# An LSTM over 512 steps: 18 instead of 19 plain steps in the head, U sums ahead of cells, raw V blocks stored later

## The chip, the cores and the metric

The kernel runs on one core of a Trainium2 chip. The metric is the device time of one execution in microseconds, the median of the runs. In names of engines, PE is TensorE, DVE is VectorE, ACT is ScalarE, POOL is GpSimd and SP is SyncE, whose queue issues all DMAs here.

## The reference

An LSTM layer with residual, batch 32, 512 steps, input and hidden size 512, float32:

```python
xW = jnp.einsum('ntd,dg->ntg', x, Wx) + b          # 32 x 512 x 2048
def step(carry, xw_t):
    prev_h, prev_c = carry
    a = xw_t + prev_h @ Wh
    i = jax.nn.sigmoid(a[:, :Hd])
    f = jax.nn.sigmoid(a[:, Hd:2 * Hd])
    o = jax.nn.sigmoid(a[:, 2 * Hd:3 * Hd])
    g = jnp.tanh(a[:, 3 * Hd:])
    next_c = f * prev_c + i * g
    next_h = o * jnp.tanh(next_c)
    return ((next_h, next_c), next_h)
return x + lstm_forward(x, cond_1024, Wx, Wh, b)   # cond_1024 is h0; c0 = 0
```

## The kernel before, in words

**Two kinds of work share PE.** The serial one: in each step t, `h_part(t)` multiplies h by Wh (32 matmuls into one PSUM bank, L272), and `cell(t)` does the gates: ACT L285 to L290 and DVE L288 to L292 in the head, ACT L298 to L305 and DVE L302 to L309 later; the transposed h (`ht`, L292 or L309) releases h_part(t + 1). POOL adds the residual (L317), and SP stores two steps' output (L321). While a cell runs, PE is filled with the other work, x times Wx.

**x times Wx in two ways.** 32 of the 512 steps are *plain*: 32 matmuls of 128x256 each (`plain_block`, L200). `HEAD` of them come first (steps 0 to 18 before), `TAIL` of them are the last steps of the sequence (13 before). The other 480 steps go in 15 *groups* of 32 by a bilinear scheme: 26 products ("slots") per group instead of 32, and each of these again by a 7-item scheme. An item is 8 matmuls (L593) and is counted as 4 *quarters*, so that a group has 26 x 7 x 4 = 728 quarters. The variable `pos` is the place in the list of items; `emit_matmuls(n)` writes n quarters.

**What the bilinear products need.** Left factors are sums of x blocks: pair sums (`pair_sum`, DVE L538 to L544) over rows of x that SP loads (`load_row`, L528), and above them *U sums* (`make_sum`, DVE L507, into one of a few `ubuf` buffers, list `free_u`). `u_ahead(n)` makes all U sums for products up to n quarters ahead. Right factors are *V sums* of Wx blocks (`v_sum`, DVE L784 and L787), made once in the head, stored to DRAM (L791) and loaded row by row into a ring of three (`load_v`, L706 for blocks taken raw from Wx, L711 for stored ones). Blocks that are raw (`V_DIRECT`) are taken from Wx at first, and copied once into the DRAM table by `store_raw` (L688), three copies per block, one per step from a given step on. For eight blocks these are 24 steps.

**What comes behind the products.** `evacuate()` takes finished items out of PSUM: copies by ACT (L659, L668, L675) and adds by DVE (L665, L669, L672). *Weight sums* (`w_op`, DVE L451, 128x1024) combine slots into output blocks in the buffers `cbuf`, `r` and one spare (buffer 9) that lies in `xnat`. `store_blocks` stores a finished block (SP L469), and `load_xw` (SP L735, four DMAs a step) brings back the x times Wx of a step two or three steps later, which ACT copies into the step's PSUM bank (L746). Biases are seeded into banks by ACT (L636).

**The order of work is written out by hand.** Each engine runs its instructions in the order of the code. In the head, `HEAD_PLAINS[t]` names the plain steps computed in step t ahead of need, `HEAD_STREAM[t]` the quarters of the first group in step t, and `jobs[t]` the DVE work of the first steps. In a step with 48 quarters or more from step 10 on (`late_cell`), two chunks of 12 and 24 quarters are written ahead of the cell, and the rest behind it; the last branch before `emit_matmuls` in the loop decides which U sums and weight sums are written in each chunk. A budget `room["dve"]` in estimated ns steers the weight sums. From step `HEAD_STEPS` = `HEAD` on a fixed rule spreads 22 to 24 quarters over each step. At the end, from step `END`, the plain steps of the tail are computed in pieces (`plain_part`, L209), 16 pieces a plain step, five pieces per step from `SPLIT` on, as long as there are any; from `SPLIT` on gates are split in halves.

Of the kernel before, what the change touches and what calls it, by code (L numbers as in the profile page):

```python
# [20 lines left out]
W = G * P  # L21
HW = G * H

HEAD = 19
GS = 32
NG = 15
TAIL = T - HEAD - NG * GS
# [10 lines left out]
STREAM0 = HEAD + GS - AHEAD  # L38
END = HEAD + GS * NG - AHEAD
SPLIT = END + 2  # L40
LATE = (452, 454, 456, 462, 464, 466, 467)

FIRST = 13
HEAD_PLAINS = ((14, 15), (16, 17), (18, 5), (6, 11), (12,), (), (7,), (8,), (9,), (10,))
HEAD_STREAM = (0, 0, 0, 0, 0, 24, 52, 52, 56, 56, 60, 60, 60, 60, 60, 56, 52, 44, 36)
HELD = 4
V_DIRECT = (2, 3, 7, 8, 15, 17, 21, 24)

# [57 lines left out]
def kernel(  # L106
# [228 lines left out]
    free_u = [2, 3, 0, 1, 4, 5]  # L335
# [197 lines left out]
    def pair_sum(g, qs):  # L533
        z = pairs_at(min(PLACES[g % 2][q] for q in qs), len(qs))
        a21, a11, a12, a22, s1, s2, s3, s4 = (z[:, :, n] for n in range(8))
        i = group(g).summed[qs[0]]
        if i == 0:
            add(s1, a21, a22)  # L538
        elif i == 1:
            sub(s2, s1, a11)  # L540
        elif i == 2:
            sub(s3, a11, a21)
        else:
            sub(s4, a12, s2)  # L544
        for q in qs:
            group(g).summed[q] += 1
        room["dve"] -= cost_dve(256 * len(qs))
# [329 lines left out]
    with tc.manual_schedule():  # L877
# [56 lines left out]
        jobs = {}  # L934
        sums = lambda *ids: [lambda i=i: v_sum(i) for i in ids]
        jobs[0] = sums(13, 14, 15, 16)
        jobs[1] = sums(17, 18, 19) + [make_seeds] + sums(20)
        jobs[2] = sums(21, 22, 23)
        jobs[3] = [lambda: pair_sum(0, (0, 1))] * 4 + sums(24)
        jobs[4] = [lambda: u_ahead(8)] + sums(25) + [lambda: u_ahead(24)]  # L940
        raws = lambda *ids: [lambda s=s: v_raw(s) for s in ids]
        jobs[5] = [lambda: u_ahead(40)] + raws(0, 7, 17, 24)
# [21 lines left out]
        for t in range(T):  # L964
# [12 lines left out]
            if last_x and t == last_x[0] + 3:  # L977
                load_x(NCHUNK - 1)
            assert last_x or t < SPLIT - 4
            if HEAD - 2 <= t < HEAD - 2 + 3 * len(V_DIRECT):  # L980
                s, d = divmod(t - HEAD + 2, 3)
                store_raw(V_DIRECT[s], d)
            if t == 2:
                load_row(0, 0)
# [12 lines left out]
            if t < HEAD_STEPS:  # L997
# [22 lines left out]
                for i, (kind, m, cs) in enumerate(chunks):  # L1020
                    if kind == "plain":
                        room["dve"] = max(room["dve"], 0.0) + PLAIN * len(cs) / 4
                        for cc in cs:
                            plain_block(m, cc, plain_bank(m), True)
                        if i == 0:
                            cell(t)
                        evacuate()
                        if cs[-1] == 3:
                            keep(m, True)
                        plains -= 1  # L1030
                        for _ in range(-(-len(todo) // (plains + 1))):
                            todo.pop(0)()
                            flush_v()
                        if not plains:
                            for f in ends.get(t, ()):
                                f()
                    else:
                        load_v_ahead()
                        store_blocks(t < HEAD - 4)
                        u_ahead(m)  # L1040
                        if i == 0:
                            room["dve"] = min(room["dve"], 1000.0) + PLAIN
                        evacuate()
                        if i <= late_cell:
                            while wqueue and (room["dve"] > 2200 or len(free_c) < 1):
                                w_op(len(free_c) < 1)
                        else:
                            row_jobs(4)
                            u_ahead(m + (40 if i == len(chunks) - 1 and 6 < t < HEAD_STEPS - 2 and len(free_u) > 1 else 24))
                            while wqueue and (  # L1050
                                room["dve"] > (-2500 if t >= 13 and any(row_of(v[1]) == 0 for v in wqueue) else 800)
                                or len(free_c) < 2
                            ):
                                w_op(len(free_c) < 2)
                            if len(free_u) > 3:
                                u_ahead(m + 44)
                        seed_banks(m)
                        if i == 0 and t + 1 in SEEDED and t + 1 != HEAD:
                            seed_step(t + 1)
                        emit_matmuls(m)  # L1060
                        room["dve"] += m * PROD / 4
                        if i == late_cell:
                            cell(t)
                            if t + 1 == HEAD:
                                seed_step(t + 1)
                            room["dve"] -= 2100.0
                            while todo and not plains and t < 10:
                                todo.pop(0)()
                                flush_v()
                        elif i > late_cell and not plains:  # L1070
                            for _ in range(-(-len(todo) // (len(chunks) - i))):
                                todo.pop(0)()
# [102 lines left out]
```

## Time and profile before

| what | us |
|---|---|
| median of 3 runs | 3082.33 (3080.94 to 3082.45) |
| the profiled execution | 3080.49 |
| its span | 3078.7 |
| PE busy | 3059.3 (99%) |
| DVE busy | 2338.9 (76%) |
| ACT busy | 1466.5 (48%) |
| granted TensorE clock | 1.00 |

Times of single instructions are us from the start of the span. Behind a row, a bracket gives how long the engine stood idle before it, and what released it: "[0.99 <-DVE ht L292]" is 0.99 us of waiting, ended by the DVE instruction at L292 that writes `ht`. An "x32" at the end of a row is a run of 32 instructions of one form, shown as one. In such rows buffer numbers are left out, and a PE row's length reaches to the modelled end of its last matmul, so that the next row starts before it.

### The profile page before, as it was taken

The numbers are of one execution on the slowest core, as the hardware profiler recorded it, in microseconds if no ns is written. First come the engines' busy times: TensorE is split into PE (matmuls) and PEld (weight loads), VectorE is DVE, ScalarE is ACT, GpSimd is POOL, SyncE is SP. The second block draws the span as 40 slices with busy tenths as digits, with TensorE's granted clock in tenths as the row PEclk, the third lists the DMA queues.
The fourth block names the chain that finished last, engine by engine and source line by source line (L and its number), as shares of the span: only waits on it lengthen the run. The fifth ranks groups of instructions, "written<-read, shape, count | busy, mean of one in ns | idle before, by whom it ended". The sixth has DMA issues, their size and how long they took to land.

```text
span 3078.7 us, 108289 instructions
## 1 busy us (share of the span) xinstructions
PE 3059.3 (99%) x43624; PEld 1652.5 (54%) x43624; DVE 2338.9 (76%) x6308; ACT 1466.5 (48%) x5474; POOL 242.9 (8%) x508
## 2 busy tenths in 40 slices
PE   9999999999999999999999999999999999999998
PEld 6755555555555555555555555555555555555675
DVE  7588787787877878778787877877778787787644
ACT  1344545444454544445445454454544445454444
POOL 0000000000000000000000000000000000000110
PEclk9999999999999999999999999999999999999999
DMA  9888878777777877778787787877878777788530
GB/s 330 294 276 282 265 251 264 245 252 246 254 259 232 265 240 260 251 236 270 240 265 245 241 268 236 270 238 247 259 246 260 240 252 262 237 269 271 159 90 18
DMA packets 320197, 753.21 MB, mean 245 GB/s; under 512 B 52176, under 2 KB 104016, under 8 KB 319184
## 3 DMA queue, kind: packets, MB, share of 16 engines
q1 hardware_dynamic: 319696, 746.28, 75.2%
q8 instruction: 344, 5.64, 0.8%
q14 instruction: 157, 1.29, 0.1%
HBM read 564.67 MB, written 184.56 MB: 243 GB/s over the span
## 4 chain that ended last, share of the span: by engine, by line
PE 97%; DVE 2%; DMA 1%; ACT 0%; issue 0%; SPq 0%; DVEq 0%; ACTq 0%
PE gbank L272 54%; PE xbank L593 33%; PE bbank L593 5%; PE xbank L272 3%; PE xbank L209 1%; PE gbank L200 1%; DMA r<-in_L_cond_Wx_dram 0%; DVE xs L787 0%; DVE ubuf L787 0%; DVE vring L787 0%; DMA vdram<-xs 0%; DVE prod L302 0%; PE bbank L200 0%; PE xbank L200 0%; DVE s L303 0%
## 5 line engine op out<-in xcount | busy, mean ns | idle before, releaser
L272 PE MATMUL gbank<-wh_sb,ht 128*32 128x512 f32 (+1 forms) x16256 | 1774.8, 575 | 3.7 <-ACT tanh_c L305 2.0
L272 PEld LDWEIGHTS gbank<-wh_sb,ht 128*32 128x32 f32 x16256 | 604.3, 110 | 828.4 <-issue 702.0
L593 PE MATMUL xbank<-vring,ubuf 128*32 128x256 f32 (+1 forms) x13584 | 852.3, 369 | 5.4 <-ACT cbuf L675 2.2
L298 ACT ACTIVATE s<-gbank 128x128 f32<-128x128 f32 x944 | 264.7, 280 | 1160.7 <-PE gbank L272 1160.1
L593 PEld LDWEIGHTS xbank<-vring,ubuf 128*32 128x32 f32 x13584 | 528.2, 110 | 297.4 <-issue 135.6
L302 DVE TENSOR_TENSOR prod<-s 128x128 f32<-128x128 f32 x988 | 283.2, 287 | 459.8 <-ACT s L299 455.4
L317 POOL TENSOR_TENSOR oc<-xnat,ht 128x128 f32<-128x128 f32 x504 | 242.7, 481 | 2797.4 <-DVE ht L309 1308.3
L305 ACT ACTIVATE tanh_c<-s 128x64 f32<-128x64 f32 x988 | 253.4, 256 | 235.9 <-DVE s L303 232.8
L309 DVE STREAM_TRANSPOSE ht<-hbuf 128x64 f32<-128x64 f32 x986 | 242.0, 245 | 73.5 <-DVE hbuf L307 2.3
L746 ACT COPY gbank<-xw 128x512 f32<-128x512 f32 x458 | 275.2, 601 | 2.1 <-DMA xw<-xwd 1.4
L303 DVE TENSOR_TENSOR s<-prod 128x64 f32<-128x64 f32 x988 | 222.4, 225 | 34.0
L307 DVE TENSOR_TENSOR hbuf<-o,tanh_c 128x64 f32<-128x64 f32 x988 | 204.3, 207 | 31.7 <-ACT tanh_c L305 31.4
L451 DVE TENSOR_TENSOR cbuf<-cbuf 128x1024 f32<-128x1024 f32 x178 | 216.4, 1222 | 0.9
L299 ACT ACTIVATE s<-gbank 128x64 f32<-128x64 f32 x944 | 217.0, 230 | 0.0
L593 PE MATMUL xbank<-vring,r 128*32 128x256 f32 (+1 forms) x3216 | 208.5, 357 | 0.0
L593 PE MATMUL xbank<-vring,xs 128*32 128x256 f32 (+1 forms) x3120 | 202.5, 356 | 0.0
L593 PE MATMUL bbank<-vring,ubuf 128*32 128x256 f32 (+1 forms) x2600 | 184.9, 342 | 0.0
L593 PEld LDWEIGHTS xbank<-vring,r 128*32 128x32 f32 x3216 | 123.2, 110 | 78.9 <-issue 46.3
L593 PEld LDWEIGHTS xbank<-vring,xs 128*32 128x32 f32 x3120 | 120.8, 110 | 57.8 <-issue 22.9
L300 ACT ACTIVATE o<-gbank 128x128 f32<-128x128 f32 (+1 forms) x493 | 148.6, 301 | 0.0
L659 ACT COPY cbuf<-xbank 128x512 f32<-128x512 f32 x228 | 132.6, 582 | 28.4 <-PE xbank L593 17.4
L593 PEld LDWEIGHTS bbank<-vring,ubuf 128*32 128x32 f32 x2600 | 101.1, 110 | 67.6 <-issue 38.7
(170 smaller groups left out, 2550.1 us busy)
## 6 DMA issues: line engine op xcount, KB each, us to landing
vring<-vdram SPq DMA_DIRECT2D x310, 896.0 KB, 6.2
xw<-xwd SPq DMA_DIRECT2D x1920, 64.0 KB, 4.5
xwd<-cbuf SPq DMA_DIRECT2D x142, 512.0 KB, 4.6
xwd<-r SPq DMA_DIRECT2D x79, 512.0 KB, 4.3
out_dram<-oc SPq DMA_DIRECT2D x255, 128.0 KB, 3.7
xnat<-in_x_dram SPq DMA_DIRECT2D x62, 512.0 KB, 5.3
xs<-in_x_grouped_dram SPq DMA_DIRECT2D x45, 512.0 KB, 4.8
vring<-vdram SPq DMA_DIRECT2D x33, 512.0 KB, 4.9
```

The costliest lines, as they stand in the source:

```text
L272: nc.tensor.matmul(dst[j * B : (j + 1) * B], state["ht"][:, k], m, start=False, stop=True, skip_group_check=True)
L298: nc.scalar.activation(s[:, u, 0:2], g[:, n_, 0:2], AF.Sigmoid)
L299: nc.scalar.activation(s[:, u, 2], g[:, n_, 3], AF.Tanh)
L302: nc.vector.tensor_mul(prod[:, u], s[:, u, 0:2], s[:, u, 2:4])
L303: add(nxt[:, u, 3], prod[:, u, 0], prod[:, u, 1])
L305: nc.scalar.activation(tanh_c[:, HALVES[u]], nxt[:, u, 3], AF.Tanh)
L307: nc.vector.tensor_mul(hbuf[:, HALVES[u]], o[:, u], tanh_c[:, HALVES[u]])
L309: nc.vector.transpose(ht[:, 2 * u : 2 * u + 2].rearrange("p q b -> p (q b)"), hbuf[:, HALVES[u]])
L317: (nc.gpsimd if t < T - 8 else nc.vector).tensor_add(oc[:, tt % 2], x_of(t), ht)
L451: op(c_of(dst), c_of(src), c_of(bb))
L593: nc.tensor.matmul(dst[j * B : (j + 1) * B, cols], left_of(gr, s, r)[:, j * B : (j + 1) * B], right_of(row, slot, RIGHT[r])[:, cols], star ...
L746: nc.scalar.copy(bank_of(t), src)
```

## The change

There are four parts. (1) `HEAD` goes from 19 to 18, so `TAIL` from 13 to 14; the steps that are counted from the end of the groups (`LATE`, `END`, `SPLIT`) come one step earlier. Plain step 18 is no longer computed in the head; step 2 computes plains 5 and 6, step 3 only 11. The 728 quarters of the first group are dealt anew over steps 5 to 17. (2) V sum 20 is written in step 2 behind the cell instead of in step 1's jobs, 23 in step 3 instead of 2, and both sums of step 3 ahead of its four pair sums. (3) The raw V blocks are stored in steps 22 to 45 instead of 17 to 40. (4) In steps with a late cell, `u_ahead(m + 16)` is called in the two chunks ahead of the cell, if more than one U buffer is free.

```diff
-HEAD = 19
+HEAD = 18
...
-LATE = (452, 454, 456, 462, 464, 466, 467)
+LATE = (451, 453, 455, 461, 463, 465, 466)
...
-HEAD_PLAINS = ((14, 15), (16, 17), (18, 5), (6, 11), (12,), (), (7,), (8,), (9,), (10,))
-HEAD_STREAM = (0, 0, 0, 0, 0, 24, 52, 52, 56, 56, 60, 60, 60, 60, 60, 56, 52, 44, 36)
+HEAD_PLAINS = ((14, 15), (16, 17), (5, 6), (11,), (12,), (), (7,), (8,), (9,), (10,))
+HEAD_STREAM = (0, 0, 0, 0, 0, 24, 48, 52, 52, 60, 64, 68, 68, 68, 64, 60, 56, 44)
...
-        jobs[1] = sums(17, 18, 19) + [make_seeds] + sums(20)
-        jobs[2] = sums(21, 22, 23)
-        jobs[3] = [lambda: pair_sum(0, (0, 1))] * 4 + sums(24)
+        jobs[1] = sums(17, 18, 19) + [make_seeds]
+        jobs[2] = sums(20, 21, 22)
+        jobs[3] = sums(23, 24) + [lambda: pair_sum(0, (0, 1))] * 4
...
-            if HEAD - 2 <= t < HEAD - 2 + 3 * len(V_DIRECT):
-                s, d = divmod(t - HEAD + 2, 3)
+            if HEAD + 4 <= t < HEAD + 4 + 3 * len(V_DIRECT):
+                s, d = divmod(t - HEAD - 4, 3)
...
                         if i <= late_cell:
+                            if late_cell and len(free_u) > 1:
+                                u_ahead(m + 16)
                             while wqueue and (room["dve"] > 2200 or len(free_c) < 1):
                                 w_op(len(free_c) < 1)
```

Three places show what moves. The first is DVE in steps 2 to 4. The rows from L288 to L292 are a cell (the first that of step 2), the three rows at L787 with `xs_79` are V sum 20, and `prod` and `hbuf` are the cell's own tiles:

```order
-L787 TENSOR_TENSOR xs_79<-r_74,vring 128x3x256
-L787 TENSOR_TENSOR xs_79<-cbuf,vring 128x3x256
-L787 TENSOR_TENSOR xs_79<-cbuf,vring 128x256
 L288 TENSOR_TENSOR prod<-s_89 128x256
 L289 TENSOR_TENSOR s_90<-prod 128x2x64
 L291 TENSOR_TENSOR hbuf<-o_91,tanh_c 128x128
 L292 STREAM_TRANSPOSE ht_95<-hbuf 128x128
+L787 TENSOR_TENSOR xs_79<-r_74,vring 128x3x256
+L787 TENSOR_TENSOR xs_79<-cbuf,vring 128x3x256
+L787 TENSOR_TENSOR xs_79<-cbuf,vring 128x256
```

V sum 20 has gone from ahead of cell(2) to behind it. A few rows on, from the end of cell(3), with V sums 23 (`ubuf`) and 24 (`vring`) and the pair sums (L538 to L544):

```order
 L292 STREAM_TRANSPOSE ht_96<-hbuf 128x128
+L787 TENSOR_TENSOR ubuf<-r_74,ubuf 128x3x256
+L787 TENSOR_TENSOR ubuf<-cbuf,ubuf 128x3x256
+L787 TENSOR_TENSOR ubuf<-cbuf,ubuf 128x256
+L787 TENSOR_TENSOR vring<-r_74,ubuf 128x3x256
+L787 TENSOR_TENSOR vring<-cbuf,ubuf 128x3x256
+L787 TENSOR_TENSOR vring<-cbuf,ubuf 128x256
 L538 TENSOR_TENSOR xs_79<-xs_79 128x4x128
 L540 TENSOR_TENSOR xs_79<-xs_79 128x4x128
 L542 TENSOR_TENSOR xs_79<-xs_79 128x4x128
 L544 TENSOR_TENSOR xs_79<-xs_79 128x4x128
```

Between cell(3) and cell(4) now stand both V sums and then the pair sums; before, it was the pair sums and then sum 24, with sum 23 ahead of cell(3). The second place is DVE in step 13. In the kernel before the two U sums (L507) stand behind the cell (L288 to L292):

```order
L288 TENSOR_TENSOR prod<-s_90 128x256
L289 TENSOR_TENSOR s_89<-prod 128x2x64
L291 TENSOR_TENSOR hbuf<-o_91,tanh_c 128x128
L292 STREAM_TRANSPOSE ht_96<-hbuf 128x128
L665 TENSOR_TENSOR r_74<-bbank,r_74 128x256
L669 TENSOR_TENSOR cbuf<-xbank_67,cbuf 128x256
L507 TENSOR_TENSOR ubuf<-r_74,xs_79 128x896
L507 TENSOR_TENSOR ubuf<-xs_79,ubuf 128x896
```

and in the changed kernel, with the adds of the evacuation (L665, L669, L672) and two weight sums (L451) between:

```order
L507 TENSOR_TENSOR ubuf<-r_74,xs_79 128x896
L507 TENSOR_TENSOR ubuf<-xs_79,ubuf 128x896
L669 TENSOR_TENSOR cbuf<-xbank_66,cbuf 128x256
L672 TENSOR_TENSOR r_74<-xbank_70,r_74 128x256
L665 TENSOR_TENSOR r_74<-bbank,r_74 128x256
L451 TENSOR_TENSOR cbuf<-cbuf,r_74 128x1024
L451 TENSOR_TENSOR r_74<-r_74,cbuf 128x1024
L288 TENSOR_TENSOR prod<-s_90 128x256
L289 TENSOR_TENSOR s_89<-prod 128x2x64
L291 TENSOR_TENSOR hbuf<-o_91,tanh_c 128x128
L292 STREAM_TRANSPOSE ht_96<-hbuf 128x128
```

The same two U sums have gone from behind the cell to ahead of it. The third place is SP around the store of the output block that lies in the spare buffer (`xwd<-xnat`), in steps 20 to 22 before:

```order
L706 DMA vring<-in_L_cond_Wx_dram 128x256
L711 DMA vring<-vdram 128x512
L321 DMA out_dram<-oc_98 128x256
L688 DMA vdram<-in_L_cond_Wx_dram 128x256
L735 DMA xw<-xwd_85 32x512 x4
L469 DMA xwd_85<-xnat 128x2x512
L688 DMA vdram<-in_L_cond_Wx_dram 128x256
L735 DMA xw<-xwd_85 32x512 x4
L469 DMA xwd_85<-cbuf 128x2x512
```

and now, in steps 19 to 21:

```order
L706 DMA vring<-in_L_cond_Wx_dram 128x256
L711 DMA vring<-vdram 128x512
L735 DMA xw<-xwd_85 32x512 x4
L321 DMA out_dram<-oc_98 128x256
L735 DMA xw<-xwd_85 32x512 x4
L469 DMA xwd_85<-xnat 128x2x512
L469 DMA xwd_85<-cbuf 128x2x512
```

The raw stores (L688) are gone from this place, and the two block stores now follow each other behind the same reload (L735). Before, ACT's next copy into that buffer (L659) comes two steps after the weight sum that fills it; now it comes one step after.

## The prediction

> **What bounds the kernel now.** I read the page first, then busy time by stage, then TensorE's timeline wherever it pauses, and what stands on VectorE (DVE), ScalarE (ACT) and the DMA queue (SP) at that moment. Times are us from the span's start. h(t) is the product with Wh that opens step t, cell(t) the gate work behind it, "quarter" a quarter of a bilinear item (`HEAD_STREAM` counts these).
>
> ```profile
> span 3078.7 us, 108289 instructions
> PE 3059.3 (99%) x43624; PEld 1652.5 (54%) x43624; DVE 2338.9 (76%) x6308; ACT 1466.5 (48%) x5474; POOL 242.9 (8%) x508
> ```
>
> TensorE (PE) works 99% of the span, so time changes only by PE work that goes or by PE pauses. By stage (columns: stretch, length, PE busy, PEld, DVE, ACT, POOL, granted clock, DMA share, GB/s):
>
> ```profile
> 71.00:225.50 154.50, 149.03 (x2256) 95.31 (x2252) 107.54 (x206) 60.37 (x167) 10.67 (x15) 1.00 0.85 293
> 225.50:260.00 34.50, 32.51 (x434) 16.16 (x428) 28.42 (x71) 15.77 (x56) 2.30 (x5) 1.00 0.82 252
> 260.00:3040.00 2780.00, 2779.81 (x39360) 1479.76 (x39356) 2132.27 (x5877) 1362.23 (x5144) 225.54 (x479) 1.00 0.76 243
> ```
>
> From 260 to 3040 PE pauses 0.19 in all: nothing to win there but work. Before 260 it pauses 5.47 and 1.99 in the two stretches shown. These are PE's pauses and the steps around them (start, length, instruction, pause and what ended it in brackets):
>
> ```profile
> 55.51 3.71 PE L200 MATMUL gbank<-r,xnat 128*32 128x256 f32 x64
> 60.21 3.64 PE L272 MATMUL xbank<-wh_sb,ht 128*32 128x512 f32 x32 [0.99 <-DVE ht L292]
> ...
> 67.12 3.71 PE L200 MATMUL xbank<-r,xnat 128*32 128x256 f32 x64
> 70.58 3.69 PE L272 MATMUL xbank<-wh_sb,ht 128*32 128x512 f32 x32
> 74.01 1.33 PE L200 MATMUL bbank<-r,xnat 128*32 128x256 f32 x20
> ...
> 105.47 0.64 PE L593 MATMUL xbank<-vring,ubuf 128*32 128x256 f32 x8 [0.80 <-ACT cbuf L675]
> ...
> 177.31 1.07 PE L593 MATMUL xbank<-vring,ubuf 128*32 128x256 f32 x16 [1.68 <-ACT xbank L636]
> ...
> 198.18 1.07 PE L593 MATMUL xbank<-vring,ubuf 128*32 128x256 f32 x16 [1.45 <-ACT cbuf L675]
> 199.90 3.64 PE L272 MATMUL gbank<-wh_sb,ht 128*32 128x512 f32 x32
> ...
> 208.72 1.50 PE L593 MATMUL xbank<-vring,ubuf 128*32 128x256 f32 x24 [0.87 <-ACT xnat L675]
> ```
>
> Start to start, a plain step costs 70.58 - 67.12 = 3.46, an h part 74.01 - 70.58 = 3.43, and a quarter 0.108 (32 products, two a quarter, from 198.18 to h(16) at 199.90). A pause costs a little more than its bracket: behind the plain step at 55.51, h(3) was due at 58.97 and came at 60.21, so 1.24 for a bracket of 0.99. I add 0.2 to the others. Now DVE beside them:
>
> ```profile
> 56.16 0.96 DVE L787 TENSOR_TENSOR xs<-r,vring 128x768 f32<-128x768 f32 x1 [0.87 <-DMA vdram<-xs]
> ...
> 104.28 2.08 DVE L507 TENSOR_TENSOR ubuf<-xs 128x896 f32<-128x896 f32 x2
> ...
> 176.11 1.09 DVE L507 TENSOR_TENSOR ubuf<-xs,ubuf 128x896 f32<-128x896 f32 x1
> ...
> 197.03 1.05 DVE L507 TENSOR_TENSOR ubuf<-r,ubuf 128x896 f32<-128x896 f32 x1
> ...
> 207.34 0.31 DVE L292 STREAM_TRANSPOSE ht<-hbuf 128x128 f32<-128x128 f32 x1
> 207.57 1.05 DVE L507 TENSOR_TENSOR ubuf<-xs,ubuf 128x896 f32<-128x896 f32 x1
> 208.54 0.41 DVE L669 TENSOR_TENSOR r<-xbank,r 128x256 f32<-128x256 f32 x1
> ...
> 209.54 1.21 DVE L451 TENSOR_TENSOR cbuf<-cbuf 128x1024 f32<-128x1024 f32 x1
> 210.67 1.22 DVE L451 TENSOR_TENSOR xnat<-cbuf,xnat 128x1024 f32<-128x1024 f32 x1
> ```
>
> The four pauses from 105.47 on bear ACT's name, but each ends about 0.1 after the end of a U sum (L507: 105.36 for the first of the two, 177.20, 198.08, 208.62), and PE's next product reads ubuf. ACT's copies were long done; the U sum stood behind cell(t) on DVE (207.34 ends the cell, 207.57 begins the sum). So the late input is the U sum. The pause at 60.21 is a cell standing behind V sum 20, which itself waited 0.87 for a store to free its room (56.16).
>
> **The change part by part.**
>
> *Work.* The head loses one plain step and one h part that stood alone, 3.46 + 3.43: **-6.9**. The bilinear steps are 480 as before. The tail gets a plain step, cut into 16 pieces that fill steps otherwise unfilled:
>
> ```profile
> 2879.77 3.66 PE L272 MATMUL xbank<-wh_sb,ht 128*32 128x256 f32 x64
> ...
> 3043.35 3.64 PE L272 MATMUL xbank<-wh_sb,ht 128*32 128x256 f32 x64
> ...
> 3065.55 3.67 PE L272 MATMUL gbank<-wh_sb,ht 128*32 128x256 f32 x64 [0.79 <-DVE ht L309]
> 3070.35 3.67 PE L272 MATMUL xbank<-wh_sb,ht 128*32 128x256 f32 x64 [1.14 <-DVE ht L309]
> ```
>
> From 2879.77 to 3043.35 lie 36 steps with five pieces, (163.58)/36 = 4.544 each; then to 3070.35 one with four and five with none, 27.00, the last of them 4.80 and the rest 4.44 in the mean. After: 40 full steps and three empty ones. 4 x 4.544 + (2 x 4.44 + 4.80) - 27.00 = **+4.9**: a step of empty PE costs nearly what a filled one does, so only part of the piece work is hidden. Work together: -2.0.
>
> *Pauses that go.* V sum 20 now stands behind cell(2): -1.24. The U sums stand ahead of the cells at the four places: -(0.80 + 1.68 + 1.45 + 0.87 + 4 x 0.2) = -5.6. The cells behind them come 1.0 to 2.1 later; cell(16) ended at 207.65 and PE still had products until 208.72 + 1.3 = 210.0, the shortest such cover, so I cost that at nothing. If that cover were gone, each U sum would cost its 1.0 again at the next h part. The last pause is at 251.21, told by these rows (PE; DVE; SP; ACT):
>
> ```profile
> 231.36 3.64 PE L272 MATMUL gbank<-wh_sb,ht 128*32 128x512 f32 x32
> ...
> 243.19 3.64 PE L272 MATMUL gbank<-wh_sb,ht 128*32 128x512 f32 x32
> ...
> 251.21 3.64 PE L272 MATMUL gbank<-wh_sb,ht 128*32 128x512 f32 x32 [2.00 <-ACT tanh_c L305]
> ```
> ```profile
> 233.49 1.22 DVE L451 TENSOR_TENSOR xnat<-cbuf,xnat 128x1024 f32<-128x1024 f32 x1
> ```
> ```profile
> 239.56 2.92 SPq L735 DMA_DIRECT2D xw<-xwd  x4
> 242.57 0.39 SPq L469 DMA_DIRECT2D xwd<-xnat  x1
> ```
> ```profile
> 245.86 0.59 ACT L659 COPY xnat<-xbank 128x512 f32<-128x512 f32 x1 [2.94 <-DMA xwd<-xnat]
> ```
>
> An output block is ready at 234.7 in the buffer xnat, but SP issues its store only at 242.57, 7.9 later, since raw V stores and four reloads of xw a step stand ahead. ACT's copy into that buffer waits 2.94 for it, and the cell behind the copy on ACT is late: 2.00 + 0.2. With the raw stores six steps later SP is freer here: -2.2. **Pauses gone: -9.0.**
>
> *Pauses that come.* (1) h(5). Behind cell(3) DVE now has V sums 23 and 24 and four pair sums ahead of cell(4):
>
> ```profile
> 64.44 0.95 DVE L787 TENSOR_TENSOR ubuf<-r,ubuf 128x768 f32<-128x768 f32 x1
> ...
> 66.52 0.42 DVE L288 TENSOR_TENSOR prod<-s 128x256 f32<-128x256 f32 x1
> ...
> 71.15 0.69 DVE L538 TENSOR_TENSOR xs<-xs 128x512 f32<-128x512 f32 x1 [2.72 <-DMA xs<-in_x_grouped_dram]
> ...
> 73.69 0.95 DVE L787 TENSOR_TENSOR vring<-r,ubuf 128x768 f32<-128x768 f32 x1
> ```
>
> A V sum is 66.52 - 64.44 = 2.08, the pair sums 73.69 - 71.15 = 2.54, a cell on DVE about 1.85 (66.52 to its end). Before, cell(3) ended at 66.52 + 1.85 = 68.4; without V sum 23 ahead of it (2.08) and the wait at 56.16 (0.87) it ends at 65.4, and cell(4) at 65.4 + 2 x 2.08 + 2.54 + 1.85 = 73.95. Step 3 has one plain step less, so PE is ready for h(5) at 58.97 + 3.43 + 3.46 + 3.43 + 3.46 = 72.75: +1.2. If the rows of x land no earlier than 71.15, it is 71.15 + 2.54 + 1.85 - 72.75 = 2.8; if the sums run 1.2 ahead of these pitches, 0; I take the sum of the pitches, as the rows' load is now issued ahead of a V store. (2) Step 15. Behind cell(14) DVE has 7 adds of 0.33 (three from 208.54 to 209.54), four pair sums (2.5), 4 weight sums of 1.13 and 2 U sums of 0.97: 11.3. The second U sum is wanted 28 + 40 quarters and an h part after the cell's place; a cell ends 4.3 after its h part (203.33 to 207.6), so there are 64 x 0.108 + 3.43 + 40 x 0.108 - 4.3 = 10.4: +0.9, between 0 and 2.5 (one more weight sum and an add ahead). (3) Denser steps 7, 8 and 11 want their V rows and U sums sooner: +0.5, from 0 to 1.7. (4) The buffer of 245.86 is now reused one step after its store is ready, not two. Ready 3.3 after h(20) as before, issued 0.4 to 2.6 later (one block of four reloads, 2.92), landed 3.3 later (242.57 to 245.86), wanted 0.3 before h(21), that is 5.7 after h(20): late by 1.3 to 3.5. A lateness of 2.94 cost 2.2, so 0.6 to 2.8 is lost. I take +1.3, near the lower end, as the raw stores are away. **Pauses that come: +3.9.** Later raw stores run beside steps 22 to 45; before, they ran to step 40 under the same reloads with PE full (2779.81 of 2780.00): nothing.
>
> A pause can also cost through the clock. The granted clock is 1.00 in all stretches above, with pauses up to 2.00, so I price none. The Trainium skill, "TensorE: Matmul & The Clock Gate", Part 1, "What's actually happening", says that PE falls to half its clock after an idle window of about 3.4 us, and needs a busy one to return. No pause in this trace is that long; by that rule a longer one at (4) would cost an estimated 1.7 more, which is no part of the sum.
>
> **Sum:** -2.0 - 9.0 + 3.9 = -7.1 on the profiled execution's 3080.49, that is 3073.4. The median of the runs, 3082.33, lies 1.84 above it, so I expect about **3075**.
>
> **The rivals.** *All waits dissolve:* the new pauses (1) to (4) are hidden. For it: each is near 1 and counted from mean durations. 3075 - 3.9 = 3071. *The U sums only swap places with the cells:* DVE, not order, was late, and h(t+1) now waits for what the product waited for. Against it: DVE is busy 107.54 of 154.50. It gives 3075 + 5.6 = 3081, no change. The same time follows if the change doesn't do what it says (fewer than two U buffers free, so no sum moves); the written order speaks against that. *Slower: the one buffer.* If SP lags in step 20 as it did (7.9), the copy in step 21 lacks one step of slack, 243.19 - 231.36 = 11.83 for two, so 5.9: a pause of 2.2 + 5.9 = 8.1 in place of 1.3, 3082; with a landing 1.3 slower, 3083. It decides from an SP lag of about 8. For it: four reloads a step still stand there; against it: the raw stores don't.
>
> **How the numbers follow.** About 0.2%, 6.2, is what a measurement here can tell from no change: faster means under 3076.2, slower over 3088.5. The forecast has 0.45 (three quarters of it under 3076.2), the first rival 0.27, the swap 0.15, the buffer 0.10 (a third of it beyond 3088), and 0.03 for something slower that I don't see. Faster 0.61, same 0.33, slower 0.06. The range goes from 3070 (below 3071, as no pause at all would give 3069) to 3082, with the swap inside and half of the buffer's case outside.
>
> **What would show it.** Right: no pause at h(3); the pauses on ACT's names in steps 7, 13, 15 and 16 gone, with L507 ending well ahead of its product; h(511) 4.9 later counted from the tail's first split step; the copy into xnat in step 21 waiting under 3.5. Wrong: brackets with "DVE ht L292" in steps 13 to 17 (swap), one pause of 6 or more near 230 to 245 (buffer), or pauses between 260 and 3040 that weren't there, which no part of this sum holds.

## The result, and the profile after

The changed kernel takes 3077.28 us (median of 22 runs, 3075.30 to 3079.47), the one before, run beside it, 3080.81 (22 runs, 3079.04 to 3083.78). The ratio is 0.9987, with a 95% interval from 0.9981 to 0.9992: 3.5 us faster, where 7.1 were forecast. That is 0.13%, clear of no change by its interval, though less than the 0.2% that the prediction took as the least to be told: it had put 0.61 on a time under 3076.2 and 0.33 on no difference by that measure, which is what came. Its profiled execution has a span of 3073.8 us, 4.9 less than before; it is one of the quicker ones.

The top of the page of the changed kernel, and its busy time by stage (columns as before: stretch, length, PE, PEld, DVE, ACT, POOL, clock, DMA share, GB/s):

```profile
span 3073.8 us, 108383 instructions
PE 3059.6 (100%) x43672; PEld 1660.7 (54%) x43672; DVE 2341.3 (76%) x6313; ACT 1464.3 (48%) x5477; POOL 240.5 (8%) x508
```
```profile
71.00:217.00 146.00, 142.37 (x2186) 88.23 (x2180) 103.81 (x198) 57.98 (x160) 7.93 (x14) 1.00 0.88 302
217.00:260.00 43.00, 41.28 (x561) 20.74 (x557) 35.57 (x94) 19.46 (x74) 3.23 (x7) 1.00 0.89 285
260.00:3035.00 2775.00, 2774.70 (x39304) 1484.32 (x39300) 2127.20 (x5863) 1357.85 (x5135) 224.41 (x478) 1.00 0.75 242
```

The middle is full as before (0.30 of pauses). PE still pauses in the head, 3.63 from 71 to 217 and 1.72 from there to 260, but at other places. These are the rows of the changed kernel's PE timeline with a pause, and the place of h(3); the pause of step 5 is as before and left out:

```profile
59.39 3.69 PE L272 MATMUL xbank<-wh_sb,ht 128*32 128x512 f32 x32
...
74.42 3.64 PE L272 MATMUL gbank<-wh_sb,ht 128*32 128x512 f32 x32 [1.01 <-DVE ht L292]
...
164.00 0.64 PE L593 MATMUL bbank<-vring,ubuf 128*32 128x256 f32 x8 [0.54 <-DVE r L665]
...
173.63 0.64 PE L593 MATMUL xbank<-vring,r 128*32 128x256 f32 x8 [0.38 <-DVE cbuf L669]
...
193.82 0.64 PE L593 MATMUL xbank<-vring,ubuf 128*32 128x256 f32 x8 [0.70 <-DVE xnat L669]
...
196.95 1.07 PE L593 MATMUL xbank<-vring,ubuf 128*32 128x256 f32 x16 [0.35 <-ACT r L659]
...
222.42 3.64 PE L272 MATMUL gbank<-wh_sb,ht 128*32 128x512 f32 x32 [0.50 <-DVE hbuf L307]
...
241.49 3.64 PE L272 MATMUL gbank<-wh_sb,ht 128*32 128x512 f32 x32 [1.22 <-DVE hbuf L307]
```

There is none at h(3) (59.39), and no U sum (L507) ends one any more. The one at h(5) (74.42) and the one at h(22) (241.49) are those that the prediction put there. New are those that end with an add of the evacuation, L665 or L669, and the cell at 222.42. DVE in the changed kernel around three of them:

```profile
161.26 1.22 DVE L451 TENSOR_TENSOR xnat<-xnat,r 128x1024 f32<-128x1024 f32 x1
162.40 1.22 DVE L451 TENSOR_TENSOR r<-r 128x1024 f32<-128x1024 f32 x1
163.53 0.42 DVE L665 TENSOR_TENSOR r<-bbank,r 128x256 f32<-128x256 f32 x1
...
190.95 1.22 DVE L451 TENSOR_TENSOR r<-cbuf,r 128x1024 f32<-128x1024 f32 x1
192.20 1.23 DVE L451 TENSOR_TENSOR cbuf<-cbuf,r 128x1024 f32<-128x1024 f32 x1
193.35 0.42 DVE L669 TENSOR_TENSOR xnat<-xbank,xnat 128x256 f32<-128x256 f32 x1
...
219.65 1.22 DVE L451 TENSOR_TENSOR r<-r 128x1024 f32<-128x1024 f32 x1
220.79 0.28 DVE L302 TENSOR_TENSOR prod<-s 128x128 f32<-128x128 f32 x1
```

Each time weight sums (L451) stand on DVE ahead of what PE wants: an add that frees a PSUM bank (163.95, and PE goes on at 164.00), another (193.77, PE at 193.82), a cell (220.79, whose ht comes late for h(19)). The h(22) chain of the changed kernel, from its DVE, SP and ACT:

```profile
229.69 1.22 DVE L451 TENSOR_TENSOR xnat<-cbuf,xnat 128x1024 f32<-128x1024 f32 x1
```
```profile
228.23 1.77 SPq L735 DMA_DIRECT2D xw<-xwd  x4
230.11 0.36 SPq L321 DMA_DIRECT2D out_dram<-oc  x1
230.87 2.21 SPq L735 DMA_DIRECT2D xw<-xwd  x4
233.18 0.39 SPq L469 DMA_DIRECT2D xwd<-xnat  x1
```
```profile
236.14 0.58 ACT L659 COPY xnat<-xbank 128x512 f32<-128x512 f32 x1 [2.16 <-DMA xwd<-xnat]
```

The block is ready at 230.9, its store is issued at 233.18 behind a block of reloads, it lands 3.0 later, and ACT's copy has waited 2.16.

To compare kernels step by step, I take each step's length from h(t) to h(t + 1) and subtract its PE work: 3.433 for h, 3.455 for each plain step, 0.1079 for each quarter (rates at which steps without a pause come out at 0.00). What is left is what the step lost, in us. The kernels e0 to e12 are the experiments below (there is no e6). "h(22)" is the loss of the step that ends with the late copy into the spare buffer: step 21, or 22 with 19 plain steps in the head.

| step | before | changed | e0 | e1 | e2 | e3 | e4 | e5 | e7 | e8 | e9 | e10 | e11 | e12 |
|---|---|---|---|---|---|---|---|---|---|---|---|---|---|---|
| 2 | 1.25 | 0 | 0 | 0 | 0 | 0.84 | 0 | 0 | 0 | 0 | 0 | 0 | 0 | 0.37 |
| 3 | 0.03 | 0 | 0 | 0 | 0 | 1.38 | 0 | 0 | 0 | 0 | 0 | 0 | 0 | 1.39 |
| 4 | 0.27 | 1.25 | 1.41 | 1.26 | 1.27 | 1.71 | 0 | 0 | 1.26 | 1.26 | 1.47 | 1.47 | 1.26 | 2.29 |
| 5 | 0.84 | 0.84 | 0.84 | 0.84 | 0.84 | 0.84 | 0.86 | 2.31 | 0.84 | 0.84 | 0.85 | 0.84 | 0.84 | 2.53 |
| 7 | 1.04 | 0 | 0 | 0 | 0 | 0 | 1.04 | 0 | 0 | 1.04 | 0 | 0 | 0 | 0 |
| 10 | 0 | 0 | 0 | 0 | 0 | 0 | 0 | 0 | 0 | 1.99 | 0 | 0 | 0 | 0 |
| 11 | 0.22 | 0.09 | 0.09 | 0.13 | 0.09 | 0.09 | 0.65 | 0.59 | 0.09 | 1.04 | 0.09 | 0.11 | 0.09 | 0.09 |
| 12 | 0.23 | 0.78 | 0.77 | 0.78 | 0.77 | 0.77 | 0.23 | 0.77 | 0.78 | 0.78 | 0 | 0.78 | 0.01 | 0.78 |
| 13 | 2.01 | 0.81 | 0.82 | 0.81 | 0.82 | 0.81 | 3.17 | 0.81 | 0.81 | 0 | 0.01 | 0.82 | 0 | 0.82 |
| 14 | 0.25 | 0.09 | 0.08 | 0.09 | 0.09 | 0.09 | 0.79 | 0.09 | 0.09 | 0.09 | 2.00 | 0.09 | 0.14 | 0.09 |
| 15 | 1.66 | 1.89 | 1.89 | 3.01 | 1.88 | 1.88 | 0.82 | 1.88 | 1.88 | 1.88 | 0 | 1.89 | 0.59 | 3.01 |
| 16 | 1.06 | 0 | 0 | 0 | 0 | 0 | 0 | 0 | 0 | 0 | 0 | 0 | 0 | 0 |
| 17 | 0 | 0 | 0 | 0 | 0 | 0 | 0 | 0 | 0 | 0 | 1.08 | 0 | 1.08 | 0 |
| 18 | 0 | 0.68 | 0.67 | 0.69 | 0.68 | 0.68 | 0 | 0.68 | 0.68 | 0.68 | 0.70 | 0.69 | 0.70 | 0.69 |
| h(22) | 2.21 | 1.43 | 2.76 | 2.02 | 4.05 | 3.12 | 1.47 | 1.72 | 1.59 | 3.07 | 1.79 | 0.84 | 0.82 | 5.11 |

Five of these traces (e2, e3, e4, e8, e12) hold a stretch in which PE ran at half its clock (see the last section). Its price stands in the table for e4 (0.9 in step 13 and 0.8 in step 14) and for e12 (1.7 in step 5); elsewhere it falls into the step behind h(22), which the table leaves out.

All steps up to h(22) together lost 11.2 before and lose 7.9 in the changed kernel's profiled execution. So where did its 4.9 come from? Work in the head: -6.9. Pauses: -3.3. Tail, by the first split h part (2870.75) and h(511) of the changed kernel:

```profile
2870.75 3.66 PE L272 MATMUL xbank<-wh_sb,ht 128*32 128x256 f32 x64
...
3065.42 3.67 PE L272 MATMUL gbank<-wh_sb,ht 128*32 128x256 f32 x64 [0.79 <-DVE ht L309]
```

That is 194.67 against 190.58: +4.1. The start, h(0) at 28.37 against 27.85: +0.5. From the end of the head to the split steps, 2629.26 against 2628.56: +0.7. The sum is -4.9, the difference of the spans.

### The profile page after: what moved, and what is told of

Read it like the earlier page. It is cut to its first block, busy times and chain, and to the rows that moved or that the text cites. A ratio compares the mean times of both kernels' runs of the same rounds, so it can differ in the third digit from the quotient of the medians.

```text
span 3073.8 us, 108383 instructions
## 1 busy us (share of the span) xinstructions
PE 3059.6 (100%) x43672; PEld 1660.7 (54%) x43672; DVE 2341.3 (76%) x6313; ACT 1464.3 (48%) x5477; POOL 240.5 (8%) x508
## 4 chain that ended last, share of the span: by engine, by line
PE 97%; DVE 2%; ACT 0%; issue 0%; DMA 0%; SPq 0%; DVEq 0%; ACTq 0%
PE gbank L272 54%; PE xbank L593 32%; PE bbank L593 5%; PE xbank L272 3%; PE xbank L209 2%; PE gbank L200 1%; PE xbank L200 1%; DVE cbuf L451 0%; DVE prod L302 0%; DVE r L451 0%; PE xbank L911 0%; DMA xw<-xwd 0%; DVE s L303 0%; PE bbank L200 0%; DVE ubuf L507 0%
## 5 line engine op out<-in xcount | busy, mean ns | idle before, releaser
L451 DVE TENSOR_TENSOR cbuf<-cbuf 128x1024 f32<-128x1024 f32 x168 | 203.5, 1218 | 0.9
L659 ACT COPY cbuf<-xbank 128x512 f32<-128x512 f32 x225 | 131.1, 582 | 21.4 <-PE xbank L593 14.7
```

What stands on the lines that cost most here:

```text
L451: op(c_of(dst), c_of(src), c_of(bb))
```

## The experiments

Each kernel was timed against the one before in five rounds on one chip; such an interval is some 0.09% wide to each side, 2.8 us, so the ratio alone hardly parts most of them. What parts them is the table above, where losses that follow from the order of instructions repeat to a few hundredths.

**e0: the changed kernel again.** 

> The changed kernel once more, as a measure of what differs from run to run. My theory: pauses that hang on the order of instructions alone (steps 4, 5, 12, 13, 15, 18: 1.25, 0.84, 0.78, 0.81, 1.89, 0.68 us) repeat within 0.05 us, and only the one that waits for a DMA (h(22), 1.43) moves by 0.5 us or more. Rival (all pauses vary, and single traces tell little): several differ by over 0.3 us. Time as before: 0.9987 of the kernel before.

3077.39 us, ratio 0.9988 (0.9980 to 0.9997). The pauses of steps 5 to 18 repeat within 0.02; that of step 4 moves by 0.16, more than expected, and that at h(22) by 1.33. In step 4 no DMA is waited for: the V sum ahead of cell(3) (L784) starts at 61.30 and at 61.34 in the two traces, while h(0) came at 28.37 and at 27.80. So DVE had worked through its sums since the start, whenever PE began. A table of losses from one trace tells orders apart to a few hundredths, except at these two kinds of places.

**e1: no U sums ahead.**

```diff
-                            if late_cell and len(free_u) > 1:
-                                u_ahead(m + 16)
```

> The changed kernel without the U sums ahead of the cells. My theory: the pauses of 5.6 us in steps 7, 13, 15 and 16 come back, and the pauses that the changed kernel has in steps 12, 13 and 15 (3.5 us by its trace: adds that free PSUM banks, standing behind weight sums) go or shrink, so 2 us slower than the changed kernel, 1.5 us faster than the one before. Rival (the U sums only swapped places with the adds, and nothing was gained by them): no slower than the changed kernel, 3.5 us faster than before.

3078.04 us, 0.9993 (0.9984 to 1.0002). By the trace both theories fall; the time alone can't tell, as the interval holds the changed kernel's 0.9987. The pauses of steps 7, 13 and 16 do not come back; only step 15 changes, from 1.89 to 3.01. In the order of instructions these two lines move one single U sum in the whole stream, in step 15. PE in this kernel:

```profile
193.31 0.64 PE L593 MATMUL xbank<-vring,ubuf 128*32 128x256 f32 x8 [0.70 <-DVE xnat L669]
...
196.73 1.93 PE L593 MATMUL xbank<-vring,ubuf 128*32 128x256 f32 x32 [1.69 <-ACT cbuf L675]
```

and its DVE, with the U sum behind the cell (L292) again, ending 0.1 ahead of the product:

```profile
195.35 0.31 DVE L292 STREAM_TRANSPOSE ht<-hbuf 128x128 f32<-128x128 f32 x1
195.58 1.05 DVE L507 TENSOR_TENSOR ubuf<-ubuf 128x896 f32<-128x896 f32 x1
```

It was the new deal of the quarters that put the other U sums ahead of the cells, since the ends of its chunks fall elsewhere; e12, which has the new deal without these lines, shows the same.

**e4: 19 plain steps and the old deal, with the other three parts.**

```diff
-HEAD = 18
+HEAD = 19
...
-HEAD_STREAM = (0, 0, 0, 0, 0, 24, 48, 52, 52, 60, 64, 68, 68, 68, 64, 60, 56, 44)
+HEAD_STREAM = (0, 0, 0, 0, 0, 24, 52, 52, 56, 56, 60, 60, 60, 60, 60, 56, 52, 44, 36)
```

> The kernel before with the other three parts: 19 plain steps in the head, the quarters dealt as before, but U sums ahead, raw stores later (from step 23) and the new order of V sums. My theory: work as before, so without the 2.8 us of the plain step that moved (6.9 out of the head, 4.1 into the tail by the trace); pauses 11.2 us before, here 2 to 6, since U sums and h(3) no longer wait and steps of 60 quarters crowd DVE less: 5 to 9 us faster than before on pauses alone, so 3 to 6 us faster than the changed kernel would only follow if its pauses come from the denser steps; I expect 4 us faster than before. Rival (the gain is the plain step's work alone): the time of before within 1 us.

3079.66 us, 0.9996 (0.9987 to 1.0005). With the old deal the two lines do move U sums ahead of the cells of four steps, 13 to 16. The pauses of steps 15 and 16 shrink by 1.9 together, but in step 13 PE now waits longer than before, for an add:

```profile
175.72 0.64 PE L593 MATMUL bbank<-vring,ubuf 128*32 128x256 f32 x8 [2.07 <-DVE r L665]
```

Behind this pause PE ran at half clock for 3.41 us (columns as in the busy time by stage; the clock is the third number from the end):

```profile
173.55:176.96 3.41, 1.34 (x28) 0.81 (x28) 2.83 (x7) 1.44 (x5) 0.45 (x1) 1.00 0.85 294
176.96:180.37 3.41, 3.41 (x32) 1.30 (x24) 3.28 (x5) 1.93 (x4) 0.00 (x0) 0.50 0.79 258
```

Half of that stretch, 1.7, is lost: 0.9 in step 13, 0.8 in step 14. Steps 7 to 16 lose 6.5 before, 6.7 here, 3.7 in the changed kernel, 4.8 in e1 and e12 (the new deal without U sums ahead). Without the half clock it would be 5.0 here. So U sums ahead of cells take 1.5 off with the old deal, which the half clock took back in this execution, and 1.1 with the new one.

The theory had this kernel 4 us faster than before; the medians differ by 0.9. Its losses by the table are 9.0 against 11.2, or 7.3 without the half clock, 3.9 less than before and near the 4 of the theory. But 6 of its 11 runs show a lower clock, against 7 of the 33 of the kernel before, and from the end of the head to the split steps its trace takes 2630.30 against 2628.56, 1.7 more. Why is open.

**e3: V sums and pair sums as before.**

```diff
-        jobs[1] = sums(17, 18, 19) + [make_seeds]
-        jobs[2] = sums(20, 21, 22)
-        jobs[3] = sums(23, 24) + [lambda: pair_sum(0, (0, 1))] * 4
+        jobs[1] = sums(17, 18, 19) + [make_seeds] + sums(20)
+        jobs[2] = sums(21, 22, 23)
+        jobs[3] = [lambda: pair_sum(0, (0, 1))] * 4 + sums(24)
```

> The changed kernel with the V sums and pair sums of steps 1 to 3 in the order of before. My theory: the pause of 1.2 us at h(3) returns, the one of 1.25 us at h(5) shrinks to 0.3, so 0.3 us slower than the changed kernel, hardly to be measured, but plain in the trace. Rival (step 3 has one plain step less, so DVE is late at h(5) in any order): h(3) 1.2 and h(5) 1.2, so 1.2 us slower.

3079.34 us, 0.9997 (0.9988 to 1.0006). Steps 2 to 4 lose 0.8, 1.4 and 1.7 us, together 3.9 against 1.25 in the changed kernel. That is more than either expectation: with one plain step less in step 3, every h part from h(3) to h(5) waits for DVE. The new order of these sums is worth 2.7 us here, and 1.5 with 19 plain steps (e4: 0.9 in steps 2 to 5, before 2.4).

**e2: raw V blocks stored early.**

```diff
-            if HEAD + 4 <= t < HEAD + 4 + 3 * len(V_DIRECT):
-                s, d = divmod(t - HEAD - 4, 3)
+            if HEAD - 2 <= t < HEAD - 2 + 3 * len(V_DIRECT):
+                s, d = divmod(t - HEAD + 2, 3)
```

> The changed kernel with the raw V stores from step 16 on, two steps ahead of the groups' end as before. My theory: SP is late again with the store out of xnat; one step less slack makes the pause at h(22) 3 to 8 us instead of 1.4, so 2 to 6 us slower than the changed kernel. Rival (SP is held by the reloads of xw, and the raw stores hardly count): the pause stays within 0.5 us of 1.4, and the time with the changed kernel's.

3078.91 us, 0.9995 (0.9987 to 1.0004). The theory holds: SP is later (ACT's copy waits 4.79), and the loss at h(22) is 4.05; on top of it the next step is 1.6 longer (see the last section). SP, ACT and PE of this kernel:

```profile
235.31 0.38 SPq L469 DMA_DIRECT2D xwd<-xnat  x1
```
```profile
238.20 0.58 ACT L659 COPY xnat<-xbank 128x512 f32<-128x512 f32 x1 [4.79 <-DMA xwd<-xnat]
```
```profile
243.54 5.23 PE L272 MATMUL gbank<-wh_sb,ht 128*32 128x512 f32 x32 [3.84 <-DVE hbuf L307]
```

**e12: the first part alone**, with `LATE` to match. Against the kernel before:

```diff
-HEAD = 19
+HEAD = 18
...
-HEAD_PLAINS = ((14, 15), (16, 17), (18, 5), (6, 11), (12,), (), (7,), (8,), (9,), (10,))
-HEAD_STREAM = (0, 0, 0, 0, 0, 24, 52, 52, 56, 56, 60, 60, 60, 60, 60, 56, 52, 44, 36)
+HEAD_PLAINS = ((14, 15), (16, 17), (5, 6), (11,), (12,), (), (7,), (8,), (9,), (10,))
+HEAD_STREAM = (0, 0, 0, 0, 0, 24, 48, 52, 52, 60, 64, 68, 68, 68, 64, 60, 56, 44)
```

> The kernel before with the first part of the change alone: 18 plain steps in the head, 14 in the tail, the quarters dealt anew; no U sums ahead of cells, raw stores two steps ahead of the groups and V sums as before. My theory now, from the runs with one part undone: the U-sum pauses of steps 7, 13 and 16 are gone by the new deal alone; there are pauses of 0.8, 1.4 and 1.7 us in steps 2, 3 and 4, 0.8 each in 12 and 13, 3.0 in step 15, 0.7 in 18 and 4 or more at h(22), 14 in all against 11.2 before; with 2.5 us less work that is the time of before within 1 us. Rival (the parts add up one by one, and this one brings at least the work): 2.5 us or more faster than before.

3082.74 us, 1.0006 (0.9997 to 1.0015). As expected: the step moved to the tail brings nothing by itself. Its losses are 17.2 against 11.2. What is more lies in steps 3 to 5, 1.7 of it by half clock, and at h(22); the other parts of the change mend both places.

**e5: V sum 24 behind cell(4).**

```diff
-        jobs[3] = sums(23, 24) + [lambda: pair_sum(0, (0, 1))] * 4
-        jobs[4] = [lambda: u_ahead(8)] + sums(25) + [lambda: u_ahead(24)]
+        jobs[3] = sums(23) + [lambda: pair_sum(0, (0, 1))] * 4
+        jobs[4] = sums(24) + [lambda: u_ahead(8)] + sums(25) + [lambda: u_ahead(24)]
```

> The changed kernel with V sum 24 behind cell(4) instead of ahead of the pair sums. My theory: DVE's 6.7 us between cell(3) and cell(4) become 4.6, so the pause of 1.25 us at h(5) goes; the U sums for the first products come 2.1 us later and may cost 0.3 us in step 5: 1 us faster than the changed kernel. Rival (cell(4) waits for the rows of x that the pair sums read, landing late, not for DVE): the pause at h(5) stays over 0.8 us, and step 5 gets worse.

3077.97 us, 0.9990 (0.9981 to 0.9999). The pause at h(5) is gone, so it was DVE's count of sums and not the rows of x; but step 5 loses 1.47 more. The pause has moved, not gone.

**e7: the reloads behind the stores in steps 18 to 29.** In the main loop the call of `load_xw` stands behind the weight sums:

```diff
+            late_reload = HEAD <= t < HEAD + 12
+            if not late_reload:
+                reload()
...
+            if late_reload:
+                reload()
```

> The changed kernel with the four reloads of xw in steps 18 to 29 issued behind the step's stores instead of ahead. My theory: the store out of xnat waits 2.35 us for SP behind the reloads of its step; without that it lands in time, ACT's copy waits under 0.3 us, and the pause at h(22) of 1.4 to 3 us goes: 1.4 us or a bit more faster than the changed kernel. Rival (the store's landing, 3.3 us, or the weight sum is late by itself): the pause stays over 1 us.

3075.62 us, 0.9982 (0.9973 to 0.9991). The pause stays, at 1.59. SP of this kernel shows why:

```profile
229.87 2.95 SPq L735 DMA_DIRECT2D xw<-xwd  x4
232.93 0.36 SPq L321 DMA_DIRECT2D out_dram<-oc  x1
233.69 0.38 SPq L469 DMA_DIRECT2D xwd<-xnat  x1
```

Now the reloads of the step before stand ahead of the store, as late as those of its own step did. Why the median is still 1.7 lower isn't shown; the interval holds the changed kernel's ratio.

**e8: a flatter deal.**

```diff
-HEAD_STREAM = (0, 0, 0, 0, 0, 24, 48, 52, 52, 60, 64, 68, 68, 68, 64, 60, 56, 44)
+HEAD_STREAM = (0, 0, 0, 0, 0, 24, 52, 56, 56, 60, 64, 64, 64, 64, 64, 60, 56, 44)
```

> The changed kernel with the first group's quarters dealt flatter: 52, 56, 56, 60, 64, 64, 64, 64, 64, 60, 56, 44 in steps 6 to 17 instead of 48, 52, 52, 60, 64, 68, 68, 68, 64, 60, 56, 44. The total is the same. My theory now: where the chunks of a step end decides which adds and sums stand ahead of which, so the pauses of steps 7 and 12 to 16 (3.6 us in all) are set by the deal: I expect the 1.6 us of steps 12 and 13 to change by more than 0.5 us either way, and new ones in steps 7, 8 and 14 of up to 2 us. Rival (68 quarters crowd DVE, flatter is better): steps 12 and 13 lose under 0.4 us, and 1 us faster in all.

3079.47 us, 0.9996 (0.9987 to 1.0005). Step 13 loses nothing, but the pause of step 7 is back with its 1.04, and steps 10 and 11 lose 3.0. PE waits for U sums again:

```profile
102.08 0.64 PE L593 MATMUL xbank<-vring,ubuf 128*32 128x256 f32 x8 [0.80 <-ACT cbuf L675]
145.03 1.50 PE L593 MATMUL xbank<-vring,ubuf 128*32 128x256 f32 x24 [1.56 <-DVE ubuf L507]
```

How dense a step is doesn't set its pause: step 10 has 64 quarters in both kernels and loses 2.0 here, and step 11 has 64 instead of 68 and loses 1.04 instead of 0.09. What is left is where the chunks end in the list of items.

**e9: weight sums held back.**

```diff
-                            while wqueue and (room["dve"] > 2200 or len(free_c) < 1):
+                            while wqueue and (room["dve"] > 3400 or len(free_c) < 1):
...
-                                room["dve"] > (-2500 if t >= 13 and any(row_of(v[1]) == 0 for v in wqueue) else 800)
+                                room["dve"] > (-2500 if t >= 13 and any(row_of(v[1]) == 0 for v in wqueue) else 2000)
```

> The changed kernel with both thresholds for weight sums in the head's steps higher (3400 for 2200 ahead of a cell, 2000 for 800 behind it), so that fewer stand ahead of the adds that free PSUM banks; in step 12 one weight sum of 1.14 us goes from ahead of an add (L665) to behind it, in step 13 two still stand ahead of the cell. My theory: the pause of 0.78 us in step 12 goes, that of 0.81 in step 13 stays, that of 1.89 in step 15 moves by up to 1 us either way, as one weight sum less stands ahead of its U sum: 1 to 2 us faster than the changed kernel. Rival (DVE is full there, and what is held back is paid for two steps later): the sum of the pauses of steps 11 to 18 (4.3 us) stays within 0.5 us.

3074.84 us, 0.9979 (0.9970 to 0.9989). With one weight sum behind the add instead of ahead, the add ends at 162.89, where it ended at 163.95:

```profile
161.34 1.22 DVE L451 TENSOR_TENSOR xnat<-xnat,r 128x1024 f32<-128x1024 f32 x1
162.47 0.42 DVE L665 TENSOR_TENSOR r<-bbank,r 128x256 f32<-128x256 f32 x1
162.80 1.22 DVE L451 TENSOR_TENSOR cbuf<-r 128x1024 f32<-128x1024 f32 x1
```

Steps 12, 13 and 15 lose nothing; 3.5 us are gone, the pause of step 13 too, which the theory had kept. That of step 18, behind another weight sum, stays. In this trace step 14 loses 2.0 instead, for a V row that lands late (its row below, from PE), and step 17 loses 1.1 for an add. So the sum of steps 11 to 18 is 3.9 against 4.3, as the rival had it, although the median fell by 2.4. The wait for the V row isn't there in e11, which has the same order at this place (0.14 in step 14).

```profile
185.55 0.64 PE L593 MATMUL xbank<-vring,r 128*32 128x256 f32 x8 [1.18 <-DMA vring<-vdram]
```

**e10: only step 20's reloads behind its stores, and four pieces a step late in the tail.**

```diff
-            late_reload = HEAD <= t < HEAD + 12
+            late_reload = t == HEAD + 2
...
-            due = 0 if t < END else max(0, 13 - n // 2) if t < SPLIT else 5
+            due = 0 if t < END else max(0, 13 - n // 2) if t < SPLIT else 5 if t < SPLIT + 32 else 4
```

(the first against e7, the second against the changed kernel)

> The changed kernel with two edits whose effects lie at different places. First, only in step 20 the four reloads of xw are issued behind the step's stores. My theory: SP reaches the store out of xnat with nothing ahead but the output store, about 2.3 us earlier, so the pause at h(22) falls from 1.4 to 2.8 us to under 0.7. Rival (something else in SP's order is late): it stays over 1.2 us. Second, from the 33rd split step on four pieces of plain work a step instead of five: ten steps of 4.46 and one empty of 4.45 in place of eight of 4.535 and three empty of 4.45, so 194.1 instead of 194.7 us from h(468) to h(511), 0.6 us less; rival: a step with four pieces costs as much as one with five, 195.1. Together 1.5 to 2.5 us faster than the changed kernel.

3074.89 us, 0.9979 (0.9970 to 0.9988). SP and ACT of this kernel:

```profile
229.77 1.56 SPq L321 DMA_DIRECT2D out_dram<-oc  x1
231.74 0.38 SPq L469 DMA_DIRECT2D xwd<-xnat  x1
```
```profile
235.02 0.58 ACT L659 COPY xnat<-xbank 128x512 f32<-128x512 f32 x1 [1.57 <-DMA xwd<-xnat]
```

The store comes at 231.74, 1.4 behind the sum's end (229.16 + 1.22 in this trace) instead of 2.3, and the loss is 0.84: between the two expectations, as the output store now holds SP. The tail is 194.57, 0.1 less and not 0.6; its steps with four pieces take 4.46 to 4.49, but its last step took 4.82 where the changed kernel's took 4.45. e11 (4.81) and the kernel before (4.80) have such a last step too, e4 (4.45) and the others not; what makes it is open.

**e11: the edits of e9 and e10 together.**

> The changed kernel with the weight sums held back, the reloads of step 20 behind its stores, and four pieces a step late in the tail, all three edits together. My theory: they act at different places, so the gains of 2.4 us each add up to 4 to 5 us against the changed kernel, 7.5 us or more faster than before; the pauses of steps 12, 13 and 15 are gone, that at h(22) under 1. Rival (both gain at the same place, h(22), by making DVE or SP earlier there): no more than 3 us faster than the changed kernel.

3072.77 us, 0.9974 (0.9963 to 0.9984). The two add up: 4.5 us faster than the changed kernel by the medians, 8.1 faster than before. Losses are 5.5, of which 1.26 at h(5) and 0.84 in step 5 are left from the changed kernel. This is the fastest version found.

## Why the prediction was half right

**Right.** PE's work in the head, -6.9. Next to nothing for denser steps: 0.5 forecast, 0.1 measured. The pause at h(3) gone. The new pause at h(5), forecast at +1.2, is a loss of 1.25, and e5 shows that it is DVE's sums. The buffer reused a step earlier: forecast a copy that waits 1.3 to 3.5 and a loss of 1.3, measured 2.16 and 1.43, and e2 shows the raw stores' share. That 1.43 lies so near is luck, as the same kernel lost 2.76 there in e0. The old U-sum pauses all went: 5.8 by the table, 5.6 forecast.

**Mis-sized: "Pauses that come".** The step put +3.9 on new pauses; the profiled execution has 6.8 (steps 4, 12, 13, 15, 18 and h(22): 1.25 + 0.78 + 0.81 + 1.89 + 0.68 + 1.43). Three of them the prediction did not have, 12, 13 and 18, 2.3 in all, and step 15 was put at +0.9, for a U sum, where it is 1.9 and its longest wait is for an add (193.82). The prediction followed only U sums and cells through DVE's order; PE also waits for the adds that free its banks, and those stood behind weight sums. "The cells behind them come 1.0 to 2.1 later", which the prediction "cost ... at nothing", was true for the cells, and passed over the adds between. e9 shows it: hold back weight sums, and the pauses of 12, 13 and 15 go. For step 18, whose cell stands behind a weight sum, it is argued from the rows alone.

**Right for a wrong reason: the U sums.** I put the end of the four pauses on U sums written ahead of the cells, as the order of the changed kernel shows them, without asking which part of the change moved them. e1 and e12 show that the new deal alone ends three of the four, and that the lines written for it are worth 1.1 us on top. With the old deal (e4) they end that of step 16 and halve that of step 15, but in step 13 the wait passes from the U sum to an add, and in that trace half clock followed the longer pause. The rival that U sums only swap places with what PE waits for was true of that step; the partner was the add, not the cell.

**Off by two odd steps: the tail.** +4.9 was forecast and +4.1 measured. The trace of before holds two odd steps there, one of 4.86 among the full ones and the last of 4.80, and I took both into the rates; the changed kernel's has none. With 4.53 and 4.45 in their place, as the steps beside them have it, the tail of before is 189.9 and the plain step adds 4.8. The tail of e4, 13 plain steps as before, is 190.25 with one such step of 4.88, and 189.9 without it. So the cost of a plain step was right; the odd steps come and go, and their cause is open.

**Not in the sum.** The start (+0.5) and the middle (+0.7). The start moves between 27.56 and 28.61 in all the traces, and the middle between 2628.6 and 2630.9, where 1.4 to 2.3 is half clock in e2, e3, e8 and e12. These and h(22), which moves by over 1 us in the same kernel, are as large as a whole term of the sum, so a single profiled execution could not have given the difference of the medians any better; which of them makes 3.5 us of the medians out of the 4.9 of the spans is open. The cause of the middle's 0.7 is open too.

**Luck.** The forecast of 3075 rests on a median of three runs, 3082.33, that lay 1.5 above that of the 22 run later. From 3080.81 the same sum gives 3073.7. So the time was missed by 2.3, but the saving, which the sum is about, by 3.6.

## What to carry to other kernels

When an engine that runs in written order is given less time, follow every kind of instruction through its order that the bound engine waits for, the small ones that free a buffer included; a wait that is taken from one of them often passes to the next in line. Before a gain is put on a part of a change, see which part moves the rows: here a table of numbers ended three of the four pauses that two lines of code were written for. And losses per step, length minus work, compare two orders to hundredths of a microsecond where the medians' intervals are about a hundred times wider, once the granted clock in those steps has been looked at.

## What the runs showed of the hardware

PE's clock falls after shorter pauses than I had thought. After the pause of 3.84 at h(22) in e2 the h part behind it took 5.23 instead of 3.64 (its row stands above), and the step was 1.6 longer. The same happened after 2.01 in e12, but not after 2.55 in e0:

```profile
76.57 5.34 PE L272 MATMUL gbank<-wh_sb,ht 128*32 128x512 f32 x32 [2.01 <-DVE ht L292]
```
```profile
242.38 3.64 PE L272 MATMUL gbank<-wh_sb,ht 128*32 128x512 f32 x32 [2.55 <-DVE hbuf L307]
```

The granted clock tells why. In all 14 traces it is 1.00 or 0.50, and from one change to the next lies a whole number of stretches of 3.41 us. Cut by these stretches, the busy time of e2, e12 and e0 around the three pauses is (two rows each; the number behind the first comma is PE's busy time, the third from the end the clock):

```profile
239.98:243.39 3.41, 0.00 (x0) 0.00 (x0) 3.23 (x9) 0.99 (x6) 0.00 (x0) 1.00 0.92 313
243.39:246.81 3.42, 3.27 (x16) 0.90 (x20) 3.35 (x7) 1.62 (x4) 0.46 (x1) 0.50 0.98 287
```
```profile
73.82:77.24 3.42, 1.41 (x23) 0.52 (x18) 2.82 (x7) 0.78 (x2) 0.65 (x1) 1.00 1.06 404
77.24:80.65 3.41, 3.41 (x20) 0.87 (x16) 3.38 (x5) 0.59 (x1) 0.56 (x1) 0.50 0.73 273
```
```profile
237.29:240.70 3.41, 2.54 (x52) 1.68 (x44) 2.77 (x4) 1.87 (x8) 0.00 (x0) 1.00 0.97 293
240.70:244.11 3.41, 1.73 (x17) 0.67 (x21) 3.20 (x11) 2.27 (x6) 0.46 (x1) 1.00 1.07 320
```

The pause of 2.01 lies within one stretch; that of 2.55 lies across two, 0.87 in one and 1.68 in the other. Between the start and the last step of the traces, seven stretches were run at half clock. In the stretch ahead of each, PE stood idle for 2.01 us or more; in no other stretch did it stand idle for more than 1.82 (e1, from 239.81). So what counts here is the idle time within a stretch, with a bound somewhere between 1.82 and 2.01 of 3.41 us, and whether a pause of 2 to 3 us passes it depends on where the stretches happen to lie. The price is half of PE's busy time in the next stretch: 3.27 / 2 = 1.6 in e2, 3.41 / 2 = 1.7 in e12.

The Trainium skill, "TensorE: Matmul & The Clock Gate", Part 1, "What's actually happening", gives about 3.4 us for the window, and half the clock after an idle one. The estimate of 1.7 from it fits the price, but a window that is idle for 2.01 of its 3.41 was enough here.

Every run lists its mean clock. In the 14 profiled executions it reads 1.0 without such a stretch behind the start, 0.999 with one and 0.998 with three. By this, 8 of the 11 runs of e2 and 10 of 11 of e12 had one or more, 7 of the 33 of the kernel before that ran beside e0, and none of e7, e10 and e11. In e1 the 4 runs with one have a median of 3080.38, the other 7 one of 3077.42. So a part of what parts the medians here is how often a pause of 2 us and more meets a stretch.
